# Constant products ahead of TensorE's waits, and the skip path mixed from an image-major load through DRAM, in layer 0 of a two-layer spectral and attention kernel

## Chip, cores and metric

One core of one Trainium2 chip. The metric is the device time of one execution in microseconds (us), as the median over several runs. All arithmetic is in 32-bit floating point.

## What is computed

The input x is [4, 32, 128, 128]: 4 groups b of 32 images t, each 128 rows (w in the kernel) by 128 columns (c). After a group norm over sets of four columns, layer 0 runs on each b: an instance norm, key, query and value made by spectral convolutions with 32 heads, attention over the 32 images of a b, a projection back to one channel with a skip, and two small spectral layers. Layer 1 is a token attention and a mixture of experts; the change does not touch it. The part of the reference that the change touches is the skip inside the attention's values and projection, which for one pixel is a mixing of the 32 images of a b:

```python
def _fno_layer(x, conv_w, skip_w, oh, ow, inner_norm=False, act=False):
    skip = jnp.einsum('bixy,oi->boxy', x, skip_w)
    skip = _fourier_resize(skip, oh, ow)
    xf = _spectral_conv(x, conv_w, oh, ow)
    if inner_norm:
        xf = _inorm(xf)
    y = xf + skip
    ...
v = _fno_layer(xn, Vcw, Vsw, H, W)
...
p_attn = jax.nn.softmax(scores, axis=-1)
av = jnp.einsum('bnts,bnsk->bntk', p_attn, vf)
...
p = _fno_layer(av, Pcw, Psw, H, W)
a = _inorm(p + xa, attn_w, attn_b)
```

## The kernel before

Layer 0 loops over b (line 687). Five engines work on queues of their own, each in its order: TensorE (PE, with its weight loads PEld), VectorE (DVE), ScalarE (ACT), GpSimd (POOL) and SyncE (SP), whose queue issues most of the DMAs. In layer 0 the order of each queue is not the order of the text: the framework's planner takes the text's order as priority, estimates durations, and issues whatever is ready on an engine, so later work can be placed ahead of earlier work that would wait. The order is fixed when the program is built. Layer 1 (line 1020 and after) has its order written out by hand.

Tiles come from pools with tags; tiles of one tag share its buffers. In PSUM the tags are "a", "b" and "wide", two buffers each (a "wide" tile may take two banks). In SBUF the tag "v" has three buffers, "pr" six, and "y", "spec", "rs", "q" one each.

The stages of one b, in the order of the text, with the names that the profile shows:

- Statistics (`image_sums`, line 319). Sums over each image by products with a one-column matrix (`rows8`, line 330), the group norm's mean `gm` and inverse deviation `gr` per column, `gs = gm * gr`, and their copy to every partition, `by_group` (lines 359 to 363): row 0 the scale, row 1 the negative offset, for 32 sets of columns.
- Spectra (`spectra_of_images`, line 418, through `forward`, line 253). Products by line 248 (`pz`) and lines 263 and 264 (`px`), the result to `xx`, and to DRAM as `xd`.
- Scores (`attention_weights`, line 486). For 17 columns yy, two products of elements, `pa` and `pb` (lines 520 to 524, VectorE or GpSimd), and four TensorE products with 32 output rows each into `sp` (line 528). Then a softmax, and the weights to DRAM and back (`prd`, `pr`, lines 572 and 577).
- Product stage (lines 748 to 788). Five blocks x0 of 13 rows of modes (the last 12), and four steps i in each. A step broadcasts a part of `xd` to 128 partitions (`xb`, line 758, four buffers), copies it to PSUM (`xw`, line 767), multiplies it with the weights `gb` four times (`u`, lines 773 on GpSimd and 775 on VectorE) and adds eight products of TensorE into `po` (line 778). Of eight multiplies in two steps, three are GpSimd's. At the end of a block `po` goes to `rs` (line 788).
- Skips (function `skips`, line 719), one piece of 16 columns behind every second step i, eight pieces in the blocks 0 to 3. A piece is 16 transposes on TensorE (`pxt`, line 723), four scalings on ScalarE (`xq`, line 733), four mixing products with the block matrix `bd` (`sk`, line 742), and one copy to `q` (line 745).
- Way back of the attention (`py` line 798, `pv2` line 273, `four` line 278): the result is added to `q` by line 811, eight adds of four images, each with its statistics.
- Two small layers: `spectra(layer, src)` (`pz` line 248, `px` line 871), `weighed` (sums of squares, closed by one product through `sums`, line 314, whose result gives the norm), and `back` (line 288: `y1` line 297, `four` line 308), with an evacuation of `y1` to SBUF between the two. Behind the first layer the exact gelu runs (lines 941 and 944); with it line 848 adds the attention's result. Behind the second, lines 999, 1006 and 1010 finish, and the images go to DRAM (`x1`).

In the text, the statistics of b + 1 stand behind the first small layer of b, its spectra and scores within the second. Before the first b they stand on their own, with the preparation of the weights beside them. `gl`, the gelu's result, and `sqx`, the squares of the first small layer, have the tag "y". The images of b + 1 are loaded at the head of iteration b (`load`, line 120), two transfers on SP's queue and two on ACT's.

## Time and profile before

| | us |
|---|---|
| median of three runs (3177.18 to 3182.71) | 3178.72 |
| profiled execution | 3191.62 |
| its span, first to last instruction | 3189.9 |
| mean granted TensorE clock, share of full | 0.953 |
| TensorE busy | 2928.7 |
| VectorE busy | 2290.9 |
| ScalarE busy | 2311.7 |
| GpSimd busy | 2102.7 |

Layer 0 ends at about 1105 us of the span; its products of line 1010 end there and layer 1's first long run of products starts. The page's second part cuts the span into 40 slices of about 80 us, one digit each: the busy share in tenths, and for PEclk the clock that was granted to TensorE in tenths of full speed. So layer 0 is the first 14 digits. A chain of waits is followed back from the last instruction, at each step to what released it. In a row of groups, "x32" counts instructions; one product of 32-bit operands is two of them in this program (640 products of line 778 are 1280 instructions). "128*32 128x429" is a product with 128 rows of weights, 32 output rows, and 429 columns. A number behind a stage's engine is busy time, and the count of instructions in brackets.

The product stage, from its first `po` product to the last copy `rs`, runs from 113.8 to 181.1 us for b = 0, from 371.5 to 439.8 for b = 1, from 639.0 to 707.5 for b = 2 and from 903.9 to 966.9 for b = 3.

### The profile page before, as it was taken

Reading aid. Unit: us, or ns where it says so; the run is one execution under the profiler, and the core shown is the slowest. Engines: PE = TensorE matmul, PEld = TensorE weight load, DVE = VectorE, ACT = ScalarE, POOL = GpSimd, SP = SyncE. Lnnn points to the kernel's source line nnn. Section 1 sums busy time; section 2 is a strip of 40 time slices with the busy share of each in tenths; the row PEclk is TensorE's granted clock in tenths of the full one; section 3 lists DMA queues with packets and bytes.
Section 4 is the critical chain, followed back from the end, with each engine's and each line's share of the span. In section 5 each row is a group of like instructions: output and inputs, shape, how many; then the busy total and the mean of one; then the engine's idle time right before and its main releaser. Section 6 shows DMA issues by size and latency. Waiting matters only on the chain.

```text
span 3189.9 us, 53099 instructions
## 1 busy us (share of the span) xinstructions
PE 2928.7 (92%) x19634; PEld 1438.2 (45%) x19634; DVE 2290.9 (72%) x5035; ACT 2311.7 (72%) x3138; POOL 2102.7 (66%) x1831
## 2 busy tenths in 40 slices
PE   7888798798888789999999999999999999999997
PEld 5366365345546444444344443444444444444443
DVE  5876666667677566777666868866778777687887
ACT  2344243253343589998999999998999999999992
POOL 1621540460451289878788797889878889888773
PEclk6998998899898799999999999999999999999998
DMA  6301310130140211010111010011010011101000
GB/s 140 111 18 30 95 50 3 49 123 1 30 130 2 57 31 31 8 31 7 31 37 24 14 24 14 8 39 31 23 29 9 14 37 24 37 1 31 14 14 14
DMA packets 152308, 112.77 MB, mean 35 GB/s; under 512 B 36878, under 2 KB 140657, under 8 KB 151441
## 3 DMA queue, kind: packets, MB, share of 16 engines
q1 hardware_dynamic: 136209, 103.61, 12.2%
q10 hardware_dynamic: 15840, 5.77, 0.8%
q8 instruction: 155, 2.54, 0.3%
q14 instruction: 104, 0.85, 0.1%
HBM read 68.37 MB, written 20.00 MB: 28 GB/s over the span
## 4 chain that ended last, share of the span: by engine, by line
PE 61%; POOL 12%; ACT 9%; DVE 9%; issue 7%; DMA 1%; ACTq 0%; POOLq 0%; DVEq 0%; SPq 0%
PE d L1446 19%; PE po L1465 11%; PE px L1352 6%; ACT r L1496 4%; PE po L778 4%; PE n L1446 3%; POOL e L1505 3%; POOL e L1504 3%; PE pz L248 2%; PE four L308 2%; ACT e L1512 2%; PE px L871 1%; PE sk L742 1%; POOL kx L1111 1%; DVE r L1501 1%
## 5 line engine op out<-in xcount | busy, mean ns | idle before, releaser
L1501 DVE TENSOR_TENSOR r<-n,r 128x1024 f32<-128x1024 f32 (+1 forms) x1056 | 961.6, 952 | 479.0 <-PE n L1446 389.4
L1504 POOL TENSOR_TENSOR e<-r 128x512 f32<-128x512 f32 x528 | 673.2, 1275 | 268.1 <-DVE r L1501 267.6
L1496 ACT ACTIVATE r<-d 128x1024 f32<-128x1024 f32 (+1 forms) x1056 | 792.9, 802 | 67.4 <-PE n L1446 56.4
L1508 ACT ACTIVATE r<-r 128x1536 f32<-128x1536 f32 x528 | 783.6, 1484 | 16.8
L1505 POOL TENSOR_TENSOR e<-e,r 128x512 f32<-128x512 f32 x528 | 671.3, 1271 | 41.4
L1446 PE MATMUL d<-qe,ke 32*128 32x512 f32 (+3 forms) x2304 | 605.8, 602 | 39.6 <-ACT r L1496 36.5
L1465 PE MATMUL po<-e,kx 128*128 128x512 f32 (+3 forms) x1152 | 594.5, 605 | 15.6 <-POOL e L1517 15.6
L1446 PE MATMUL n<-qe,ke 32*128 32x512 f32 (+3 forms) x2304 | 606.2, 601 | 0.0
L1446 PE MATMUL n<-qf,kf 32*128 32x512 f32 (+3 forms) x2304 | 552.6, 554 | 0.0
L1446 PE MATMUL d<-qf,kf 32*128 32x512 f32 (+3 forms) x2304 | 550.2, 553 | 0.0
L1356 DVE SCALAR_TENSOR_TENSOR xc<-px,wgt,xc 128x128 f32<-128x128 f32 x1024 | 358.1, 350 | 42.2 <-PE px L1352 9.7
L1512 ACT ACTIVATE e<-e 128x512 f32<-128x512 f32 x528 | 325.8, 617 | 66.2 <-POOL e L1505 65.6
L1465 PEld LDWEIGHTS po<-e,kx 128*128 128x128 f32 x1152 | 175.5, 188 | 392.8 <-issue 306.9
L1446 PEld LDWEIGHTS d<-qe,ke 32*128 32x128 f32 x2304 | 176.5, 183 | 359.3 <-ACT r L1496 339.5
L773 POOL TENSOR_TENSOR u<-xb,gb 128x858 f32<-128x858 f32 (+1 forms) x120 | 233.1, 1968 | 139.5 <-PE po L778 128.0
L1446 PEld LDWEIGHTS d<-qf,kf 32*128 32x128 f32 x2304 | 220.2, 186 | 176.1 <-issue 163.8
L1352 PE MATMUL px<-we,x2t 128*128 128x512 f32 x512 | 264.0, 601 | 6.8 <-DVE xc L1356 6.0
L775 DVE TENSOR_TENSOR u<-xw,gb 128x858 f32<-128x858 f32 (+1 forms) x200 | 206.6, 1082 | 59.2 <-PE po L778 46.6
L885 POOL TENSOR_TENSOR spec<-part,part 128x512 f32<-128x512 f32 x16 | 24.8, 1550 | 333.4 <-ACT z L188 75.2
L1446 PEld LDWEIGHTS n<-qf,kf 32*128 32x128 f32 x2304 | 228.3, 185 | 19.2 <-issue 11.4
L778 PE MATMUL po<-u,pr 128*32 128x429 f32 (+1 forms) x1280 | 191.1, 548 | 26.8 <-DVE u L775 11.7
L524 POOL TENSOR_TENSOR pb<-xm 128x1024 f32<-128x1024 f32 x48 | 90.7, 1913 | 159.1 <-ACT xm L457 152.8
(388 smaller groups left out, 3953.9 us busy)
## 6 DMA issues: line engine op xcount, KB each, us to landing
xb<-xd SPq DMA_DIRECT2D x128, 214.5 KB
xc<-x SPq DMA_DIRECT2D x29, 512.0 KB
x<-x SPq DMA_DIRECT2D x16, 512.0 KB
qf<-qe SPq DMA_DIRECT2D x64, 128.0 KB
out<-xc SPq DMA_DIRECT2D x15, 512.0 KB
xb<-xd SPq DMA_DIRECT2D x32, 198.0 KB
gb<-gd SPq DMA_DIRECT2D x4, 1056.0 KB
x<-in_x SPq DMA_DIRECT2D x8, 512.0 KB
```

The lines of the kernel that those rows point to most:

```text
L773: nc.gpsimd.tensor_tensor(u, xb, gk, ALU.mult)
L778: nc.tensor.matmul(po[32 * j : 32 * j + 32], pr[:, i, k], u[:, r], start=i == 0 and k == 0, stop=i == 3 and k == 1,)
L1352: nc.tensor.matmul(px, x2t[:, k * P : (k + 1) * P], we[:, e0 : e0 + 4], start=True, stop=True)
L1356: nc.vector.scalar_tensor_tensor(xc[:, k], px[:, e], wgt[:, k, e0 + e : e0 + e + 1], xc[:, k], ALU.mult, ALU.add)
L1446: nc.tensor.matmul(o, k, q, start=turn == 0 or g > 0, stop=turn == 1 or g > 0)
L1465: nc.tensor.matmul(sums[c, h][:, q0 : q0 + c1 - c0], kx[:, jb], e[:, c0:c1], start=jb == 0, stop=is_last and q0 > 2 * P, skip_group_check= ...
L1496: nc.scalar.activation(r[:, g], d, AF.Ln, scale=1.0 / DSCALE)
L1501: nc.vector.tensor_tensor(r[:, g], part, r[:, g], ALU.mult)
L1504: nc.gpsimd.tensor_tensor(e, r[:, 1], r[:, 2], ALU.add)
L1505: nc.gpsimd.tensor_tensor(e, e, r[:, 0], ALU.add)
L1508: nc.scalar.activation(r, r, AF.Exp, scale=-1.0)
L1512: nc.scalar.activation(e, e, AF.Exp)
```

## The change

A helper `hold(tile, n)` issues n products of two constant matrices (`rows` and 128 columns of `inv`) into a PSUM tile that nobody reads. They have no input that is computed. The change puts them

- 18 ahead of the product that makes `by_group`, for b = 0;
- 4 ahead of each of the 17 turns of the score loop, into a PSUM tile `beside` of the tag "b";
- 26 and 8 ahead of the two `cm` products, for b = 0, and 14 ahead of the first `po` of every b;
- 24 ahead of the sum that closes `weighed` for `v0`, and for `v1` in the last b;
- 3 in each `back`, ahead of its first `four`.

The skips are made in another way. The group's offset in `by_group` is now the mean alone (`gm`, not `gs`), since the scale is applied afterwards. The images of b are loaded a second time, as `xs`: partition 32 j + t holds rows 32 j to 32 j + 31 of image t, 16 KB of contiguous memory, in four DMAs of 512 KB behind the broadcasts of block 0. A piece is now four rows of each of the four partition groups, all columns: one product of `bd` with 512 columns of `xs`, one of `bd` with the group offsets (read with repetition), and one multiply on VectorE that scales the sum and puts it back in `xs`. The piece goes to DRAM (`qd`, 256 KB), by SP's queue. The eight pieces stand in the blocks 1 to 4. When all are written, `q` is read back in four DMAs of 512 KB; an order without a wait puts them behind the last broadcast of the stage. The load of the images of b + 1 moves from the head of the iteration to behind this read. `xs` has the tag "y".

```diff
--- before.py
+++ after.py
@@ -287,7 +287,6 @@
     def back(spec, a, take):
-
         wide = [ps.tile([P, 2, 512], F32, name="y1", tag="wide") for _ in range(2)]
         for slot in range(4):
             c = slice(slot * P, slot * P + P)
@@ -305,12 +304,22 @@
             v = grp.tile([P, 4, C], F32, name="v1", tag="v", bufs=3)
             evacuate(v.rearrange("p k c -> p (k c)"), wide[g // 2][:, g % 2])
             four = ps.tile([P, 4, C], F32, name="four", tag="b")
+            if g == 0:
+                hold(four[:, 0], 3)
             nc.tensor.matmul(four, inv, v, start=True, stop=True)
             take([image(a, g, k) for k in range(4)], four)
-    def sums(name, matrix, src):
-
-        m = ps.tile(list(src.shape), F32, name=name, tag="wide")
+    def hold(tile, n):
+
+        for _ in range(n):
+            nc.tensor.matmul(tile, rows, inv[:, : tile.shape[-1]], start=True, stop=True)
+
+    def sums(name, matrix, src, idle=0):
+
+        m = ps.tile([P, P] if idle else list(src.shape), F32, name=name, tag="wide")
+        if idle:
+            hold(m, idle)
+            m = m[:, : src.shape[-1]]
         nc.tensor.matmul(m, matrix, src, start=True, stop=True)
         return m
@@ -358,8 +367,10 @@
         both = small.tile([P, 2, 32], F32, name="both", tag="both")
         nc.vector.tensor_scalar(both[:, 0], of_group, gr, None, ALU.mult)
-        nc.vector.tensor_scalar(both[:, 1], of_group, gs, -1.0, ALU.mult, ALU.mult)
+        nc.vector.tensor_scalar(both[:, 1], of_group, gm, -1.0, ALU.mult, ALU.mult)
         by_group = small.tile([P, 2, 32], F32, name="by_group", tag="by_group")
+        if b == 0:
+            hold(ps.tile([P, P], F32, name="early", tag="wide"), 18)
         nc.vector.tensor_copy(by_group, sums("bg", ones, both))
         n = 1 + 2 * KY
         colg = small.tile([P, 2, n], F32, name="colg", tag="colg")
@@ -511,7 +522,9 @@
         )
         sp = ps.tile([P, T, 16], F32, name="sp", tag="b")
+        beside = ps.tile([P, P], F32, name="beside", tag="b")
         for yy in range(KA):
+            hold(beside, 4)
             xs_p = xp[:, yy].unsqueeze(2).to_broadcast(tt)
             xs_s = xm[:, yy].unsqueeze(2).to_broadcast(tt)
             pa = grp.tile(tt, F32, name="pa", tag="pr", bufs=6)
@@ -688,8 +701,6 @@
         xt = loaded
         by_group, _, _, ysc = normed
         xd = front[2]
-        if b + 1 < B:
-            loaded = load(b + 1)
         ph, pr = weights
@@ -700,6 +711,8 @@
         for h in range(2):
             r = slice(32 * h, 32 * h + 32)
             cm = ps.tile([P, T, 16], F32, name="cm", tag="a")
+            if b == 0:
+                hold(cm.rearrange("p s t -> p (s t)")[:, :P], 26 - 18 * h)
             nc.tensor.matmul(cm, pv[r].to_broadcast([NH, P]), ph[r], start=True, stop=True)
             cd = grp.tile([P, T, 16], F32, name="cd", tag="v", bufs=3)
             nc.vector.tensor_tensor(cd, cm, sel.unsqueeze(2).to_broadcast([P, T, 16]), ALU.mult)
@@ -715,47 +728,46 @@
             ALU.mult,
         )
         q = big.tile([P, T, C], F32, name=f"q_{b}", tag="q")
-
-        def skips(c0):
-            px = ps.tile([P, 4, P], F32, name="pxt", tag="a")
-            for k in range(4):
-                for j in range(4):
-                    nc.tensor.matmul(
-                        px[32 * j : 32 * j + 32, k],
-                        xt[:, :, c0 + 4 * k + j],
-                        ident,
-                        start=True,
-                        stop=True,
-                    )
-            xq = grp.tile([P, 4, P], F32, name="xq", tag="v", bufs=3)
-            for k in range(4):
-                g = c0 // 4 + k
-                nc.scalar.activation(
-                    xq[:, k],
-                    px[:, k],
-                    AF.Identity,
-                    bias=by_group[:, 1, g : g + 1],
-                    scale=by_group[:, 0, g : g + 1],
+        rows_of_4 = "t (j w) c -> j t w c"
+        qd = dram.tile([T, H, C], F32, name=f"qd_{b}")
+        xs = big.tile([P, H // 4, C], F32, name=f"xs_{b}", tag="y")
+
+        def load_by_image():
+            for j in range(4):
+                nc.sync.dma_start(
+                    out=xs[32 * j : 32 * j + 32], in_=x[b, :, 32 * j : 32 * j + 32]
                 )
-            sk = ps.tile([P, 16, T], F32, name="sk", tag="b")
-            for k in range(4):
-                nc.tensor.matmul(
-                    sk[:, 4 * k : 4 * k + 4], xq[:, k], bd, start=True, stop=True
-                )
-            nc.scalar.copy(q[:, :, c0 : c0 + 16], sk.rearrange("w c t -> w t c"))
-
-
+
+        def skips(w0):
+
+            r = slice(w0, w0 + 4)
+            sk = ps.tile([P, 4, 32, 4], F32, name="sk", tag="b")
+
+            def over_pixels(t):
+                return t.unsqueeze(1).unsqueeze(3).to_broadcast([P, 4, 32, 4])
+
+            nc.tensor.matmul(sk, bd, xs[:, r], start=True, stop=False)
+            nc.tensor.matmul(sk, bd, over_pixels(by_group[:, 1]), start=False, stop=True)
+            nc.vector.tensor_tensor(
+                xs[:, r].rearrange("p w (g k) -> p w g k", k=4),
+                sk,
+                over_pixels(by_group[:, 0]),
+                ALU.mult,
+            )
+            nc.sync.dma_start(out=qd.rearrange(rows_of_4, j=4)[:, :, r], in_=xs[:, r])
         rs = big.tile([P, KX, KY], F32, name=f"rs_{b}", tag="rs")
-        at_c = 0
+        at_w = 0
         for x0 in range(0, KX, NK):
             nk = min(NK, KX - x0)
             m = nk * KY
             po = ps.tile([P, NK * KY], F32, name="po", tag="a")[:, :m]
+            if x0 == 0:
+                hold(po[:, :P], 14)
             for i in range(4):
                 xb = late.tile([P, 2, NK * KY], F32, name="xb", tag="xb")[:, :, :m]
                 for r in range(2):
-                    nc.sync.dma_start(
+                    last_xb = nc.sync.dma_start(
                         out=xb[:, r],
                         in_=xd[8 * i : 8 * i + 8, r, x0 : x0 + nk]
                         .rearrange("s x y -> s (x y)")
@@ -782,11 +794,25 @@
                                 start=i == 0 and k == 0,
                                 stop=i == 3 and k == 1,
                             )
-                if i % 2 and at_c < C:
-                    skips(at_c)
-                    at_c += 16
+                if x0 and at_w < H // 4:
+                    skips(at_w)
+                    at_w += 4
             nc.scalar.copy(rs[:, x0 : x0 + nk].rearrange("p x y -> p (x y)"), po)
-        if b + 1 == B:
+            if x0 == 0:
+                load_by_image()
+        for g in GROUPS:
+            back_in = nc.sync.dma_start(
+                out=q[:, g : g + GI], in_=qd[g : g + GI].rearrange("t w c -> w t c")
+            )
+            tc.add_manual_dep(
+                back_in.ins,
+                last_xb.ins.name,
+                mybir.DependencyInfo(mybir.DependencyClass.NoSync, mybir.DependencyReason.DATA),
+                reason="order",
+            )
+        if b + 1 < B:
+            loaded = load(b + 1)
+        else:
             for p in reversed(right):
                 p.__exit__(None, None, None)
         yf = big.tile([P, T, 2, KY], F32, name=f"yf_{b}", tag="spec")
@@ -891,7 +917,7 @@
                 nc.scalar.activation(spec[:, s4, :64], spec[:, s4, P:], AF.Copy, scale=-1.0)
             return spec, sq
-        def weighed(name, sq, squares, weights):
+        def weighed(name, sq, squares, weights, idle):
             t = sq[:, 1]
             by_row, by_column = weights
@@ -913,14 +939,14 @@
                 ALU.mult,
             )
             nc.vector.scalar_tensor_tensor(by_t, squares, by_column, by_t, ALU.mult, ALU.add)
-            m = sums("ms", ones, by_t)
+            m = sums("ms", ones, by_t, idle)
             out = per_image(name)
             nc.vector.tensor_copy(out, m)
             return out
         spec, sq = spectra(0, q)
-        v0 = weighed("v0", sq, squares, layers[0][2])
+        v0 = weighed("v0", sq, squares, layers[0][2], 24)
         nc.vector.tensor_mul(v0, v0, r2)
         nc.vector.tensor_mul(v0, v0, r2)
         r0, ve = inv_std("r0", v0)
@@ -967,8 +993,8 @@
         spec, sq = spectra(1, gl)
         if b + 1 < B:
             front = spectra_of_images(b + 1, loaded, normed)
-        v1 = weighed("v1", sq, squares, layers[1][2])
-        vc = weighed("vc", sq, squares, layers[1][3])
+        v1 = weighed("v1", sq, squares, layers[1][2], 24 * (b + 1 == B))
+        vc = weighed("vc", sq, squares, layers[1][3], 0)
         r1, _ = inv_std("r1", v1)
         s1 = par[:, S1 : S1 + 1]
         nc.vector.tensor_mul(vc, vc, r1)
```

## Prediction

> **What bounds the kernel now.** I first read the page's slices, then busy time by stage, then the chain that ended last inside one stage, then the groups of that stage. In the slices the first third of the run (layer 0, to about 1105 us) looks unlike the rest: the granted TensorE clock is often below full.
>
> ```profile
> PE   7888798798888789999999999999999999999997
> DVE  5876666667677566777666868866778777687887
> PEclk6998998899898799999999999999999999999998
> ```
>
> By stage (columns: span, then busy us and count for PE, PEld, DVE, ACT, POOL, then granted clock, DMA share, GB/s):
>
> ```profile
> 32.00:66.00 34.00, 32.41 (x148) 31.64 (x148) 15.72 (x59) 3.43 (x8) 0.00 (x0) 0.50 0.52 114
> 114.00:181.00 67.00, 64.71 (x640) 30.95 (x635) 50.24 (x50) 37.61 (x80) 54.28 (x28) 0.96 0.30 98
> 228.00:238.00 10.00, 9.08 (x73) 5.71 (x76) 8.75 (x41) 3.79 (x7) 0.00 (x0) 0.50 0.00 1
> ```
>
> Here are three kinds of stage. From 32 to 66 us (spectra of the first 32 images, b = 0) TensorE is the bound and runs at half clock, with VectorE idle half the time. From 114 to 181 us (the product stage, lines 748 to 788) it is the bound at full clock. From 228 to 238 us (the way back of the first small layer) TensorE is at half clock but VectorE is nearly full beside it, so a faster TensorE gives only part. The same pair of instructions in the chain, cold and warm, shows what the clock is worth:
>
> ```profile
> 33.25 0.43 PE px L263 x2
> ...
> 282.89 0.22 PE px L263 x2
> ```
>
> One pair of steps i of the product stage, from the chain of b = 1 (start us, us, what):
>
> ```profile
> 397.08 1.69 PE po L778 x17
> 398.77 0.33 PE pxt L723 x3
> 399.10 0.27 PE po L778 x3
> 399.37 0.87 PE pxt L723 x28
> 400.25 0.04 issue
> 400.28 0.91 PE po L778 x2
> 401.19 0.70 PE sk L742 x4
> 401.89 0.85 PE po L778 x6
> 402.74 0.42 PE sk L742 x2
> 403.16 0.84 PE po L778 x2
> 404.00 0.42 PE sk L742 x2
> ```
>
> Nothing but TensorE is on it: 7.34 us, of which po 4.56, the skips' transposes (pxt) 1.20 and their mixing (sk) 1.54. What stands next is read in the groups of 113 to 182 us:
>
> ```profile
> L773 POOL TENSOR_TENSOR u<-xb,gb 128x858 f32<-128x858 f32 (+1 forms) x28 | 54.3, 1970 | 23.6 <-PE po L778 23.1 <-DMA xb<-xd 0.6
> L775 DVE TENSOR_TENSOR u<-xw,gb 128x858 f32<-128x858 f32 (+1 forms) x47 | 49.0, 1090 | 14.4 <-PE po L778 14.3
> ```
>
> A pair has three products on GpSimd (3 x 1.97 = 5.9 us) and five on VectorE (5 x 1.09 = 5.5 us). Both wait for TensorE now, but both are close behind it.
>
> [...] with TensorE idle from 222.3 to 228.6 us the clock falls to 0.50 and stays there to 238, and the pair above takes 0.43 instead of 0.22 us. [...]
>
> **The change, part by part.** The sum is made against the profiled execution (3191.6 us, span 3189.9), which is 0.4% above the median of the runs shown (3178.7); I take the same microseconds off the median.
>
> *Skips, TensorE.* Per piece, 16 transposes and four mixing products go (1.20 + 1.54 = 2.74 us); two products of 512 columns come. The nearest row is the warm four L308: two products in 1.99 us (245.24 us in the chain). So a pair with a piece goes from 7.34 to about 6.6 us. Pieces now lie in blocks 1 to 4 instead of 0 to 3. The last block has none today and takes 10.7 us (170.4 to 181.1), close to its GpSimd products, so block 0 should drop to about 11.5 and the last rise to about 12.5. The stage: 11.5 + 3 x 13.2 + 12.5 = 63.6. A second way: po 10 x 4.56 plus 8 x 1.99 = 61.5 of TensorE alone; VectorE has 50.2 + 8 x 0.68 = 55.7 (a 128x512 add from PSUM, L811, takes 0.68), GpSimd 54.3. I take 62. Now it is 67.3, 68.3, 68.5 and 63.0 us (first po to last rs, b = 0 to 3), so the gain is 5.3 + 6.3 + 6.5 + 1 = **19**. Bounds: 63.6 gives about 13, 58 (GpSimd and VectorE bound) gives 35.
>
> *Skips, ScalarE.* Four xq and one q copy go (4 x 0.46 + 0.59 = 2.4 us a piece). ScalarE is at 37.6 of 67 us: nothing by itself, but TensorE's waits for xq go with it.
>
> *Skips, DMA.* Added per b: 2 MB of xs in, 2 MB of qd out, 2 MB of q in. The stage moves 98 to 136 GB/s now; with 6 MB more in 62 us it is about 200, against 298 to 347 GB/s seen at 4 to 12 us. The xs load is issued behind the first block, but its buffer (tag y) is free long before, so it should lie in front. The q read starts when the last piece is written, about 2.5 us after the stage (the prd write took 2.45). Four reads of 512 KB at about 180 GB/s land 3 us apart: the first at +7, the last at +16 us. The first add into q comes 16 us after the last rs (439.8 to 456.1), hidden by py and pv, and the eight adds take some 12 us more. Cost 0; without that cover about 10 us each. The load of the next images moves from in front of the stage to behind the q read. Today it delays the broadcasts once (9.80 us for one, at 375.9 us, little of it in block 0's 13.9 us); it is wanted only 70 us later. I count nothing.
>
> *New waits on SP's queue.* Each qd write waits for its multiply, and the broadcasts queued behind it wait too, on them the copies, the products and po. Four broadcast buffers, about 13 us ahead, cover it if the planner keeps later broadcasts in front of the write. I count 0; not below, since a wait adds nothing.
>
> *Group bias.* both[:,1] needs gm instead of gs: it executed at 30.36 us though gr came at 25.2, so TensorE's by_group product (30.64) can start earlier: **-1.5**.
>
> *Constant products, b = 0.* One constant product is a 128-column pair: 0.22 us warm (as px), 0.43 cold. Eighteen fill 4 us between 23 and 30.6 us, where the clock fell. Then 32.4 us of cold work becomes 16.2, with VectorE's 15.7 partly behind it; b = 1 needs about 22 us for this, part of it cold. 34 to 21: **-13** (-6 if VectorE's order binds, -16 at best). The 26, 8 and 14 products around cm and po fill 101 to 113 us, where TensorE is idle anyway: **-1.5** from a cold first pair.
>
> *Constant products before v0.* Twenty-four (5.3 us) fit the 6.3 us of waiting. Cold work behind it: b = 1 has 20.6 us of it from 493.0 to 513.7, half of which is 10; beside VectorE I take 7. b = 0: 9.6 us cold, but VectorE 8.75 of 10 busy: 2.5. b = 2: only 771 to 777 us: 2. b = 3: 3.5. **-15** (0 to -24). Those ahead of v1 in the last b come before a 13 us wait of TensorE: 0. The three per way back fit in the 0.6 us evacuation: 0.
>
> *Constant products in the score loop (line 528).* 17 x 4 x 0.22 = 15 us of TensorE. For b = 0 the loop is VectorE's (27 us, 1.4 a turn), and 0.9 + 1.1 us a turn is more: **+5**. For b = 1 to 3 GpSimd sets it (34 us, four 2.37 us additions in it): +1 each. **+8** (0 to +25).
>
> Sum: -19 - 1.5 - 13 - 1.5 - 15 + 8 = **-42**: 3149.6 for the profiled execution, **3137** for the median.
>
> **Rivals.**
> *No gain in the product stage.* With GpSimd at 5.9 and VectorE at 5.5 + 0.7 a pair, the in-order queues may lock at 7 us. Then -42 + 19 = -23: 3156. For it: both are within 1.5 us of TensorE; against it: both wait on po, 23.1 and 14.3 us.
> *Constant products spent early.* They have no inputs, and the planner moves ready work forward (sc of line 540 runs at 70.35 us, ahead of line 528's products at 72.2). If they are spent in small gaps, the long waits stay cold: -42 + 13 + 1.5 + 15 = -12: 3166. Against it for b = 0: TensorE has little else between 23 and 30 us.
> *More clock than counted.* All cold bounds and GpSimd-bound product stages: -35 - 19 - 24 = -78: 3101.
> *Slower: SP's queue.* If the qd writes stand in front of the next broadcasts, each of 32 pieces exposes part of a broadcast's landing. Its bounds are 2.0 us (the pr read) and 9.8 us (broadcast under load). At 3 us, +96 - 42 = +54: 3233. It decides from 42/32 = 1.3 us a piece. Against it: broadcasts are issued four buffers ahead now, and ready work goes first.
>
> **How the numbers follow.** Forecast 0.58; no stage gain 0.15; spent early 0.07; more clock 0.09; slower 0.08; balanced to nothing 0.03. About 0.2% (6 us) is what a measurement tells from no change. Range 3098 to 3175: it takes in all but the slower case and the nought. Faster 0.89, same 0.03, slower 0.08.
>
> **What would show it.** Right: clock 1.0 between 32 and 60 us with px pairs at 0.22; product stages of 60 to 64 us with pairs near 6.5; no wait of the q additions on a DMA; a score loop of b = 0 near 32 us. Wrong: broadcasts that land after their copies are due and SP waiting for the multiply (slower rival); pairs still above 7 us with GpSimd on the chain; clock 0.50 still at 228 or 485 us.

## The result, and the profile after

The changed kernel is **slower**, by 1.2%: 3214.44 us (median of four runs, 3213.43 to 3230.11) against 3179.22 us (median of four, 3177.18 to 3182.71); ratio 1.0121 [1.0089, 1.0153]. Here and below a ratio is to the kernel before, run beside the other, and the brackets hold its 95% interval. The profiled execution took 3230.11 us (span 3228.3), 15.7 above its median; that of the kernel before lies 12.4 above its own. So stages of the two traces may be set side by side, but a difference of some 10 us in one place needs a second trace. The mean granted TensorE clock of the profiled execution rose from 0.953 to 0.971, and the time rose too.

The slices of after. The first third has more clock than before, and TensorE is busier in it:

```profile
PE   7989989988998889999998999999999999999997
PEclk8999999999999899999999999999999999999998
```

The same three kinds of stage after the change (span, then busy us and count for PE, PEld, DVE, ACT, POOL, then clock, DMA share, GB/s):

```profile
37.00:64.00 27.00, 26.05 (x174) 25.75 (x174) 15.46 (x56) 5.67 (x10) 0.00 (x0) 0.75 0.55 118
131.00:199.00 68.00, 57.22 (x350) 14.34 (x344) 50.16 (x54) 21.25 (x41) 51.36 (x28) 0.92 0.52 166
246.00:256.00 10.00, 7.27 (x80) 4.58 (x80) 9.70 (x45) 5.99 (x13) 0.00 (x0) 0.93 0.00 0
```

In the product stage TensorE's work did fall, from 64.71 to 57.22 us, and ScalarE's from 37.61 to 21.25. But the stage took 68 us as before: TensorE now idles in it, and its clock falls to 0.92. The way back (third line) has its clock, and VectorE is full, 9.70 of 10 us.

The chain through the product stage of b = 1, where the piece shown before was TensorE alone, now has three broadcasts in it:

```profile
397.56 10.84 DMA xb<-xd
...
410.75 1.88 POOL u L785
412.62 0.04 issue
412.67 0.91 PE po L790 x4
...
427.49 1.48 DMA qd<-xs
...
430.98 11.02 DMA xb<-xd
...
448.11 10.03 DMA xb<-xd
```

The first of the three was issued ahead of every write of qd of this b (the first is at 412.11 us), behind the writes of the finished images of b = 0 (x<-x) and two loads of the next images. The planner still put these loads in front of most broadcasts (at 396.44 us), though in the text they now stand behind the read of q. The kernel before had such a broadcast too (9.80 us at 375.9 us). The other two stand among the writes of qd, and are new.

The groups of 130 to 200 us, the stage of b = 0 (busy us, mean ns of one, then idle us and what ended it), say who waits: ScalarE's copies xw, for broadcasts, 28.4 us in this one stage.

```profile
L785 POOL TENSOR_TENSOR u<-xb,gb 128x858 f32<-128x858 f32 (+1 forms) x28 | 51.4, 1857 | 33.2 <-PE po L790 29.4 <-DMA xb<-xd 2.7 <-DVE u L787 0.9
L787 DVE TENSOR_TENSOR u<-xw,gb 128x858 f32<-128x858 f32 (+1 forms) x46 | 45.5, 1031 | 14.8 <-ACT xw L779 8.6 <-PE po L790 6.0
L779 ACT COPY xw<-xb 128x429 f32<-128x429 f32 (+1 forms) x34 | 17.4, 515 | 48.9 <-DMA xb<-xd 28.4 <-DVE u L787 20.2
```

The second loss is in the score loop. The chain of b = 1 from the end of the spectra; "beside" is the tile of the constant products:

```profile
322.83 3.81 PE beside L315 x18
326.64 2.06 PE so L514 x30
...
328.76 2.88 PE beside L315 x24
331.64 1.00 PE sp L541 x8
332.63 0.42 PE beside L315 x2
333.05 0.99 PE sp L541 x8
...
337.07 1.31 PE beside L315 x10
```

TensorE is the whole chain up to the last sp product, which ends at 366.8 us. From the first sp product (331.64 us) its pieces add up to 20.8 us of sp and 14.0 us of constant products; the loop had taken 31.7 us.

By stages, summed over the four b, the two traces differ as in the first two rows below; the other rows are the experiments of the next section. "Time" is the median in us, the rest is read from the one trace of each kernel. "Score" is from the last px product of the spectra to the last sp product; "to po" from there to the first po product (b = 0 alone); "stage" from the first po to the last rs; "back" from there to the last px of the next b (of b = 3 to the end of layer 0).

| kernel | time | score | to po, b = 0 | stage | back |
|---|---|---|---|---|---|
| before | 3179 | 145.4 | 16.4 | 272.3 | 522.5 |
| after | 3214.4 | 179.7 | 23.0 | 284.5 | 508.4 |
| e1 no constants in the loop | 3195.6 | 149.0 | 20.1 | 284.5 | 504.7 |
| e2 no constants | 3199.4 | 146.3 | 22.1 | 289.6 | 506.4 |
| e3 constants only | 3202.7 | 177.3 | 22.1 | 268.3 | 499.3 |
| e4 qd by partition | 3207.9 | 177.9 | 22.9 | 253.5 | 522.9 |
| e5 qd on ScalarE's queue | 3224.3 | 177.8 | 23.0 | 284.4 | 501.1 |
| e6 broadcast on 16 | 3195.6 | 177.3 | 23.0 | 254.2 | 501.6 |
| e7 fast qd, fewer constants | 3164.8 | 142.7 | 27.2 | 256.7 | 502.1 |
| e8 constants but in the loop | 3176.2 | 147.2 | 19.2 | 263.7 | 502.4 |
| e9 half the loop's constants | 3198.7 | 157.9 | 18.5 | 288.2 | 498.1 |
| e10 skips alone, fast qd | 3165.6 | 144.2 | 20.8 | 255.7 | 506.0 |
| e11 e7, xs behind pr | 3159.9 | 144.3 | 16.4 | 261.5 | 508.6 |
| e12 e11, broadcast on 16 | 3166.7 | 144.3 | 16.3 | 259.0 | 504.3 |
| e13 first constants alone | 3180.6 | 143.8 | 20.3 | 271.6 | 503.5 |
| e14 e13 and ahead of my | 3182.5 | 142.4 | 26.6 | 269.9 | 508.7 |
| e15 e11 without constants | 3171.4 | 145.3 | 22.9 | 266.7 | 506.0 |

The kernel before, run beside each set, had medians of 3179.9 (e1 to e4), 3176.5 (e5 to e8), 3178.5 (e9 to e12) and 3183.9 us (e13 to e15); so kernels of different sets are compared by their ratios. Layer 1 takes 2084 to 2089 us in every trace. Of the 37.9 us that layer 0 ends later after the change, 34.3 are the score loops, 12.2 the stages, 6.6 the way to po of b = 0, 0.7 the same of the other b; -1.8 the first spectra, -14.1 the ways back.

### The profile page after: what moved, and what is told of

Its sections match the earlier page's. It is cut to its first block, busy times and chain, and to the rows that moved or that the text cites. A ratio compares the mean times of both kernels' runs of the same rounds, so it can differ in the third digit from the quotient of the medians.

```text
span 3228.3 us, 52967 instructions
## 1 busy us (share of the span) xinstructions
PE 3017.4 (93%) x19578; PEld 1484.6 (46%) x19578; DVE 2303.7 (71%) x5067; ACT 2249.0 (70%) x2978; POOL 2092.1 (65%) x1831
## 4 chain that ended last, share of the span: by engine, by line
PE 63%; POOL 11%; DVE 9%; ACT 8%; issue 5%; DMA 4%; SPq 0%; ACTq 0%; POOLq 0%; DVEq 0%
PE d L1472 18%; PE po L1491 11%; PE px L1378 6%; ACT r L1522 4%; PE n L1472 3%; DMA xb<-xd 3%; PE pz L248 3%; POOL e L1531 3%; PE sp L541 3%; POOL e L1530 3%; PE beside L315 2%; PE four L309 2%; PE po L790 2%; POOL u L785 2%; PE px L897 2%
## 5 line engine op out<-in xcount | busy, mean ns | idle before, releaser
L1522 ACT ACTIVATE r<-d 128x1024 f32<-128x1024 f32 (+1 forms) x1056 | 792.8, 802 | 68.4 <-PE n L1472 56.4
L1538 ACT ACTIVATE e<-e 128x512 f32<-128x512 f32 x528 | 325.8, 617 | 66.1 <-POOL e L1531 65.4
L785 POOL TENSOR_TENSOR u<-xb,gb 128x858 f32<-128x858 f32 (+1 forms) x120 | 221.6, 1866 | 174.4 <-PE po L790 109.3
L779 ACT COPY xw<-xb 128x429 f32<-128x429 f32 (+1 forms) x160 | 82.3, 515 | 240.5 <-DMA xb<-xd 122.7
L787 DVE TENSOR_TENSOR u<-xw,gb 128x858 f32<-128x858 f32 (+1 forms) x200 | 197.4, 1031 | 56.1 <-ACT xw L779 38.8
L1472 PEld LDWEIGHTS n<-qf,kf 32*128 32x128 f32 x2304 | 228.2, 185 | 19.1 <-issue 11.4
L790 PE MATMUL po<-u,pr 128*32 128x429 f32 (+1 forms) x1280 | 176.4, 579 | 48.1 <-POOL u L785 33.0
```

The lines of the kernel that those rows point to most:

```text
L785: nc.gpsimd.tensor_tensor(u, xb, gk, ALU.mult)
L790: nc.tensor.matmul(po[32 * j : 32 * j + 32], pr[:, i, k], u[:, r], start=i == 0 and k == 0, stop=i == 3 and k == 1,)
L1472: nc.tensor.matmul(o, k, q, start=turn == 0 or g > 0, stop=turn == 1 or g > 0)
L1522: nc.scalar.activation(r[:, g], d, AF.Ln, scale=1.0 / DSCALE)
L1538: nc.scalar.activation(e, e, AF.Exp)
```

## Experiments

The theory ahead of the runs: the score loop became TensorE's through the constant products, and the product stage waits for broadcasts because the writes of qd and the broadcasts share few DMA engines. Its rivals: the constant products cost little and disturb in another place; SP's queue in order holds the broadcasts back; the bytes are too many.

**e1: the loop's constant products taken out.**

```diff
-        beside = ps.tile([P, P], F32, name="beside", tag="b")
         for yy in range(KA):
-            hold(beside, 4)
```

> The changed kernel without the four constant products a turn in the score loop (line 528). Theory (they stand on the chain of a loop that TensorE now sets; the four loops took +12.3, +6.5, +8.1 and +7.4 us): about 34 us come back, 3180, level with the kernel before; the loop of b = 0 ends about 28 us after its first products, as before. Rival (the loops are longer for another cause, the later start of the work ahead or VectorE's order, and the products only fill gaps): under 8 us, 3207 to 3215.

Measured: 3195.58 us, 1.0047 [1.0031, 1.0062]. The theory holds for the loops: they are back at 149.0 us, 30.7 less in the traces. In time it does not hold in full: 18.9 us come back in the medians, of some 34 expected. So the loop is a large loss, but with it gone 15.7 us remain: there is a second one.

**e2: the new skips without any constant product; e3: the constant products on the kernel before.**

```diff
-            hold(beside, 4)
...
-            hold(ps.tile([P, P], F32, name="early", tag="wide"), 18)
...
-                hold(cm.rearrange("p s t -> p (s t)")[:, :P], 26 - 18 * h)
...
-                hold(po[:, :P], 14)
...
-                hold(four[:, 0], 3)
...
-        v0 = weighed("v0", sq, squares, layers[0][2], 24)
+        v0 = weighed("v0", sq, squares, layers[0][2], 0)
```

(e3 has the opposite lines, put into the kernel before.)

> The changed kernel with all constant products taken out, in every place; the new skips stay. What the new skips are worth alone against the kernel before. Theory (the writes of qd and the broadcasts share few DMA engines, the stages give +0.7, +6.2, +2.8, +3 us): slower than before by 8 to 16 us, 3187 to 3195. Rival (it is the constant products that moved the stages into a worse order, and the skips gain the 19 us of the forecast): 3160.

> The kernel before with all constant products put in, its own skips kept. Theory (score loops +34, cm and po of b = 0 about +5, against some -2 for the first spectra and -6 for the way back of layer 0): about +25 to +31 us, 3204 to 3210. Rival (the constant products pay for themselves as in the forecast, -13 -1.5 -15 + 8 = -21): 3158.

Measured: e2 3199.39 us, 1.0057 [1.0037, 1.0078], its stages 289.6 us; e3 3202.68 us, 1.007 [1.005, 1.009], its loops 177.3 us. Each half of the change loses by itself, some 20 us each. The mechanisms of the theory are seen in both; in time e2 lost more than the range said (19.5 us) and e3 a little less (22.8 us).

**e4: qd laid out as the partitions of xs.**

```diff
-        qd = dram.tile([T, H, C], F32, name=f"qd_{b}")
+        qd = dram.tile([P, H // 4, C], F32, name=f"qd_{b}")
...
-            nc.sync.dma_start(out=qd.rearrange(rows_of_4, j=4)[:, :, r], in_=xs[:, r])
+            nc.sync.dma_start(out=qd[:, r], in_=xs[:, r])
...
-        for g in GROUPS:
-            back_in = nc.sync.dma_start(
-                out=q[:, g : g + GI], in_=qd[g : g + GI].rearrange("t w c -> w t c")
-            )
+        for j in range(4):
+            js = slice(32 * j, 32 * j + 32)
+            back_in = nc.sync.dma_start(out=q[js], in_=qd[js].rearrange("t w c -> w t c"))
```

> The changed kernel with qd laid out as the partitions of xs have it (128 rows of 16 KB), so that a write's outer dimension is 128 and not 4; q is read back in four reads by band of rows, not by images. The bytes, the instructions that multiply and the waits of SP's queue are the same. Theory (a write whose outer dimension is 4 runs on 4 DMA engines, and the broadcasts beside it on 8, the same ones among them, so that these few are full while the mean share is 0.43): the product stages fall by 2 to 6 us each, 8 to 20 in all, 3195 to 3206, and the mean DMA share of the stage falls less than the broadcasts' landing does. Rival (SP's queue in order: the broadcasts behind a write wait for its multiply): no change within 4 us, perhaps +3 to +8 because the first addition into q now waits for all four reads.

**e5: the write of qd from ScalarE's queue.**

```diff
-            nc.sync.dma_start(out=qd.rearrange(rows_of_4, j=4)[:, :, r], in_=xs[:, r])
+            nc.scalar.dma_start(out=qd.rearrange(rows_of_4, j=4)[:, :, r], in_=xs[:, r])
```

> The changed kernel with the 32 writes of qd issued from ScalarE's queue instead of SP's; their layout stays (outer dimension 4). No broadcast stands behind a write's wait any more, but the bytes and the DMA engines that they need are the same. Theory (few DMA engines): the product stages stay long, within 3 us each of the changed kernel's 68.0, 74.5, 71.3 and 70.7 us, and the copies wait for broadcasts as much as before; 3208 to 3220. Rival (SP's queue in order holds the broadcasts back): the stages fall to 61 to 66 us, as they did with the other layout, 3185 to 3190.

**e6: broadcasts with an outer dimension of 16.**

```diff
-                        .unsqueeze(1)
-                        .to_broadcast([8, 16, m]),
+                        .unsqueeze(0)
+                        .to_broadcast([16, 8, m]),
```

(with gb and pr in the same order of partitions)

> The changed kernel with the order of the partitions of xb, gb and pr turned (head outside, image inside), so that a broadcast's source has an outer dimension of 16 with step 0 and not of 8; pr is read in 8 pieces instead of 2. qd's layout stays. Theory (few DMA engines): if the stepless outer dimension of 16 spreads a broadcast over 16 engines, the broadcasts' part on the four engines of the qd writes halves, the stages fall by 4 to 8 us each, 3190 to 3200; if the spread goes by something else, nothing. Rival (the bytes themselves, 150 to 180 GB/s, are what the stage can get): no change within 5 us.

Measured: e4 3207.9 us, 1.0082 [1.0057, 1.0106]; e5 3224.28, 1.0164 [1.0144, 1.0184]; e6 3195.55, 1.0061 [1.004, 1.0082]. In time e4 and e5 lie somewhat above their ranges, e6 within. The stages in sum: 253.5, 284.4 and 254.2 us against 284.5. What the copies xw waited for between 100 and 1015 us (count, then busy and mean ns, then idle and what ended it), one fence each for after, e4, e5 and e6:

```profile
L779 ACT COPY xw<-xb 128x429 f32<-128x429 f32 (+1 forms) x160 | 82.3, 515 | 240.5 <-DMA xb<-xd 122.7 <-DVE u L787 73.7 <-DVE pa L535 36.1
```

```profile
L778 ACT COPY xw<-xb 128x429 f32<-128x429 f32 (+1 forms) x159 | 81.5, 516 | 152.3 <-DVE u L786 127.1 <-DMA xb<-xd 16.6 <-issue 3.8
```

```profile
L779 ACT COPY xw<-xb 128x429 f32<-128x429 f32 (+1 forms) x159 | 81.6, 516 | 203.9 <-DMA xb<-xd 122.0 <-DVE u L787 78.5 <-DVE v L190 2.1
```

```profile
L780 ACT COPY xw<-xb 128x429 f32<-128x429 f32 (+1 forms) x159 | 81.5, 516 | 151.6 <-DVE u L788 113.9 <-DMA xb<-xd 29.6 <-issue 3.8
```

The wait for broadcasts (DMA xb<-xd) is 122.7 us, and stays 122.0 when the writes leave SP's queue, but falls to 16.6 or 29.6 when the shape of either transfer changes with its bytes unchanged. This clears SP's queue (e5) and the bytes (e4, e6). What is left is how a transfer is spread over the DMA engines.

The trace has no column by engine, but it has the start and the duration of every DMA packet, so the packets in flight can be counted, here every 0.02 us and where none but those of qd writes and broadcasts are in flight. From 143 to 199 us of after, with packets of a qd write (outer dimension 4) alone in flight, there are 4 of them in 236 of 254 samples. Of the broadcasts (outer dimension 8) alone, in the product stage of b = 0 of the kernel before, 8 is the most frequent count. With both in flight in after it is 8 again, in 514 of 1028 samples, and hardly ever more than 10; on engines of their own they would often be 12 (4 and 8, an estimate from these counts). So by the counts they share, as e4's expectation had it. In e4 a write (outer dimension 128) has up to 15 packets in flight, and in e6 broadcasts alone (16) have most often 16. In the views this is the DMA share, the last number but one: 0.28 with a write alone and 0.52 with both (after), 0.48 with a broadcast alone (before). Of the 16 engines that the share is a mean of, these are 4.5, 8.3 and 7.7. The traces go no further: what sets the number of engines of a transfer, and which ones it gets, was not shown.

```profile
157.80:159.00 1.20, 1.20 (x12) 0.23 (x4) 1.01 (x2) 0.30 (x1) 0.49 (x1) 1.00 0.28 104
173.30:174.80 1.50, 0.93 (x8) 0.16 (x8) 1.15 (x2) 0.00 (x0) 1.50 (x2) 1.00 0.52 163
166.08:166.94 0.86, 0.86 (x4) 0.23 (x2) 0.65 (x1) 0.00 (x0) 0.86 (x1) 1.00 0.48 179
```

Widening either transfer is enough: each gave 30 us in the stages, more than was expected of e4 and within what was expected of e6. The mean share over a longer stretch hides all this: in after the stretch 143 to 188 us, full of waits for DMA, shows a share of only 0.44 at 155 GB/s; in e4, 136 to 180 us, it is 0.58 at 182 GB/s with few of them.

e4's time fell by 6.5 us only, since "back" rose to 522.9 us. In e4 all four reads of q are due before the first addition. No addition waits for a DMA in its trace, but their order is another: for b = 0 the first comes 14.9 us behind the last rs, 12.5 in after. With the reads in 16 pieces (e7) "back" is 502.1 us; that the reads set the order is likely, and not shown by itself.

**e7: the fast qd (the layout of e4), read back by band and images in 16 pieces, no constants in the loop nor around cm and po.**

```diff
-        for g in GROUPS:
+        for g, j in ((g, j) for g in GROUPS for j in range(4)):
+            js = slice(32 * j, 32 * j + 32)
+            ts = slice(32 * j + g, 32 * j + g + GI)
             back_in = nc.sync.dma_start(
-                out=q[:, g : g + GI], in_=qd[g : g + GI].rearrange("t w c -> w t c")
+                out=q[js, g : g + GI], in_=qd[ts].rearrange("t w c -> w t c")
             )
...
-            hold(beside, 4)
...
-                hold(cm.rearrange("p s t -> p (s t)")[:, :P], 26 - 18 * h)
...
-                hold(po[:, :P], 14)
```

> The changed kernel with qd by partition (as in the run before), read back in 16 pieces by band and images so that the first addition waits for four of them, and without the constant products in the score loop and around cm and po; those of the first spectra and of the way back stay. Theory: from 3208 (qd by partition, read by band) the loops give back about 31, the products around cm and po of b = 0 about 2, the read by images about 10 of the 17 us that the ways back of layer 0 had lost: 3160 to 3172, faster than the kernel before by 0.3 to 0.6%. Rival (the gains overlap: GpSimd and VectorE set the score loop and the stage, and only part comes back): 3175 to 3190, no gain over the kernel before.

Measured: 3164.77 us, 0.9959 [0.9948, 0.997], as the theory said: 0.4% faster than the kernel before, "back" at 502.1 us. Yet b = 0 took 27.2 us to its first po. The chain there:

```profile
105.42 9.32 DMA prd<-ph
...
114.83 2.58 DMA pr<-prd
117.42 0.00 issue
117.42 2.05 PE sk L744 x2
119.47 3.00 PE po L783 x13
```

The write of prd took 2.45 us in the kernel before. Three of the four loads of xs stand on SP's queue ahead of it, and a skip's product stands ahead of the first po.

**e10: the new skips alone, with the fast qd.** The edit is e7's, with all constant products out.

> The new skips without any constant product, with qd by partition, read back in 16 pieces. It tests the forecast's -19 for the product stage with the few DMA engines out of the way. Theory: the stages are those of the forecast, 61 to 66 us, 10 to 20 us in sum below the kernel before, of which b = 0 gives 5 back ahead of its first po (the load of xs stands in front of ph's round trip): 3163 to 3172. Rival (the constant products, not the layout, made the short stages of the last runs): 3180 or more.

Measured: 3165.61 us, 0.996 [0.9951, 0.997]; stages 62.0, 63.5, 64.1 and 66.1 us. This comes close to the forecast's product stage (62), without a single constant product. It also prices the products that e7 still has, at the first spectra and in the ways back: the mean clock is 0.968 in the median of e7 and 0.958 in that of e10, and the ratios are the same.

**e11: xs and the next images behind; e12: with the broadcasts on 16.**

```diff
+                tc.add_manual_dep(
+                    by_band.ins,
+                    last_pr.ins.name,
...
+            tc.add_manual_dep(
+                first.ins,
+                last_po.ins.name,
...
-            loaded = load(b + 1)
+            loaded = load(b + 1, last_xb)
```

(order on the queues only, no waits; by_band is the load of xs, first a skip's first product; the two reads of pr also change queues, so that the last one is on SP's)

> The kernel with qd by partition and no constant products in the loop nor around cm and po, and in addition the loads of xs put behind the read of pr, the load of the next images behind the last broadcast, and the first product of a skip behind the last po product ahead of it in the program. Theory (in b = 0 the write of prd took 9.32 us beside the loads of xs, 2.45 in the kernel before, and a skip's product of 2.05 us stood ahead of the first po): b = 0 gives 7 to 9 us, the rest nothing: 3154 to 3160. Rival (the stages get longer because the skips start later and the DMA has more to do within them): 3160 to 3170.

> The run before it on this list, with the broadcasts on an outer dimension of 16 as well. Theory (with qd off the few engines nothing waits for a broadcast any more; the stages are GpSimd's, VectorE's and TensorE's): within 4 us of it. Rival (broadcasts on 8 engines still bound the stage): 4 to 12 us faster.

Measured: e11 3159.86 us, 0.9948 [0.9931, 0.9964], the lowest ratio of all, though its interval overlaps those of e7 and e10; e12 3166.73, 0.9966 [0.9955, 0.9978]. In e11 b = 0 needs 16.4 us to po, as in the kernel before, but the stages grow by 4.8 us against e7: a broadcast behind the loads takes 9.43 us. Theory and rival both hold in part. e12's median is 6.9 us above e11's, not within 4, but the intervals overlap; the broadcasts on 16 add nothing that can be told once qd is spread.

**e9: half the loop's constant products.**

```diff
-            hold(beside, 4)
+            hold(beside, 2)
```

> The changed kernel with two constant products a turn in the score loop instead of four. From the last px product to the last sp product the four batches took 145.4 us in sum in the kernel before and 179.7 after. Theory (in the loop of b = 1 TensorE has 20.3 us of sp products and 14.9 us of constant ones, 35.2, against 31.7 us that GpSimd needs; half the constant ones give 27.8, so GpSimd sets b = 1 to 3 again, and only the products ahead of the loop and b = 0, where VectorE needs 25, still cost): 150 to 156 us in sum. Rival (each constant product costs the same wherever it stands): 162 us in sum. In time: 3192 to 3200 against 3199 to 3206.

Measured: 3198.73 us, 1.0066 [1.0043, 1.009]; score 43.5, 37.8, 38.5 and 38.1 us, 157.9 in sum, above the theory's 150 to 156, through b = 0. For b = 1 to 3 this is the kernel before (37.9, 38.1, 37.8): GpSimd, busy all through these loops (28.2 of 28.2 us), sets their end again, and the half that is left is free. The tile `beside` is still there, so it was not the buffer that it takes. For these loops the cost has a threshold and is not a price a piece. b = 0 did not follow, and TensorE's order in e9 says why:

```profile
80.60 0.49 PE L315 MATMUL cm<-cst 128*128 128x128 f32 x2
81.02 0.62 PE L541 MATMUL sp<-pa,w_re 128*32 128x512 f32 x2
...
92.97 1.60 PE L315 MATMUL cm<-cst 128*128 128x128 f32 x12
```

The products meant for cm have no computed inputs, and the planner put 29 of the 34 into this loop. In e1 and e8, without any product meant for the loop, all but two moved likewise, in front of the loop of b = 0 or into it, and its score is 5.4 and 4.2 us above the kernel before; in after none did.

**e8: the constant products, but for the loop's, on the kernel before** (e3 with the line of e1 taken out).

> The kernel before with its own skips and all constant products but those in the score loop. It tests the forecast's -13 (first spectra) and -15 (way back) without the loop's cost. Theory (the way back gains about 14 us, as the stages of the run with all constant products show, 296 against 311 us in sum; the first spectra end 6 us earlier but VectorE, busy 25.5 of 26 us in the loop behind them, takes most of it back; cm and po of b = 0 cost about 6): -8 to -14, 3166 to 3172. Rival (the forecast: -13 -1.5 -15 = -29): 3150. Rival (the constants give nothing beyond what they cost): 3178 to 3182.

Measured: 3176.24 us (20 runs), 0.9988 [0.9975, 1.0001]: at most a quarter of a percent gained, perhaps nothing. Theory and forecast both fail; the rival that the constants give nothing beyond what they cost comes nearest. Layer 0 in before and in e8 (the clock is the third number from the end):

```profile
0.00:1105.60 1105.60, 934.24 (x7868) 563.73 (x7868) 764.94 (x1928) 433.14 (x915) 395.65 (x216) 0.87 0.21 59
```

```profile
0.00:1092.50 1092.50, 965.45 (x8420) 598.52 (x8420) 767.10 (x1928) 434.11 (x915) 395.90 (x216) 0.93 0.22 59
```

The clock rises from 0.87 to 0.93, and the median time hardly follows. In the trace the ways back are 20.1 us shorter and the stages 8.6, but from the last sp to the first po it takes 18.0 us more over the four b. Which of this is the products' doing isn't shown.

**e13: the first 18 products alone; e14: with 36 more ahead of my.** In the changed kernel TensorE's order in b = 0 was

```profile
22.70 4.26 PE L315 MATMUL early<-cst 128*128 128x128 f32 x36
26.80 0.33 PE L323 MATMUL bg<-both,ones 128*128 128x64 f32 x2
26.97 1.33 PE L248 MATMUL pz<-cst,x 128*128 128x128 f32 x10
35.91 0.66 PE L323 MATMUL my<-y,ones 128*128 128x64 f32 x2 [7.60 <-DVE y L396]
```

The long wait, 7.60 us, comes behind the products. In the kernel before TensorE had waited 4.47 us right ahead of bg, where they now stand.

```diff
+        if b == 0:
+            hold(ps.tile([P, P], F32, name="early2", tag="wide"), 36)
         my = sums("my", ones, y12)
```

> The kernel before with only the 18 constant products ahead of the group norm's second product (bg), b = 0. Theory (the long wait is the one for my, which comes behind them): the px products are still at 0.43 us a pair for their first third, the spectra end 4 to 6 us earlier than before (65.8), the score loop of b = 0 ends 3 to 5 us earlier; in time -5 to 0. Forecast: spectra end 13 us earlier.

> The run before it on this list with 36 further constant products ahead of my, where TensorE waited 7.60 us in the changed kernel: at 0.22 us each they fill 8 us. Theory (that wait is what lets the clock fall): px pairs at 0.22 us from the start, the spectra end at 53 to 56 us, 10 to 13 us earlier than before; but the score loop behind, where VectorE is busy 25 of 26 us, ends at 90 to 93 us, at most 7 us earlier: in time -7 to -2. Rival (the clock falls for another reason than that wait): px pairs at 0.43 us in the first third as in the run before it, and the same end.

Measured: e13 3180.62 us, 0.999 [0.9978, 1.0003], spectra to 60.4 us; e14 3182.45 us, 0.9995 [0.9985, 1.0005], spectra to 56.4. In e14 the clock is 1.00 from 32 to 56 us and the spectra take 21 us, which is the forecast's own figure; so that wait is what let the clock fall. The times show no change that can be told, against 2 to 7 us expected of e14. Its score loop ends at 87.6 us, 9.8 earlier than before, and the first po comes at 114.2 (before: 113.8). The chain of e14:

```profile
71.97 11.01 DMA xd<-xx
...
90.68 6.37 DMA xb<-xd
97.08 0.04 issue
97.12 0.52 ACT xw L779
97.64 0.52 ACT spt L548
98.16 0.04 issue
98.21 1.91 PE sc L559 x2
```

The copy of the scores (spt) stands behind two copies xw on ScalarE's queue; these wait for the first broadcasts, and they stand on SP's queue behind the last writes of xd, seventeen small loads and two of the next images. That DMA chain sets the pace of b = 0, not the spectra.

**e15: e11 without constants.**

> The fastest kernel so far (qd by partition, xs behind the read of pr, 3160 us) without any constant product. Theory (the constant products that are left raise the clock but not the pace, which VectorE and GpSimd set): within 5 us of it, 3155 to 3165. Rival (they are worth the forecast's 13 and 15 us where nothing else is in the way): 3180 or more.

Measured: 3171.41 us, 0.996 [0.9944, 0.9975]; e11 had 0.9948 [0.9931, 0.9964]. The median lies between the ranges of theory and rival, and the intervals overlap: no worth of the constant products can be told. The first po of b = 0 comes at 110.1 us in both traces.

One thing in this trace qualifies e13 and e14. Without any constant product, it has its first spectra at full clock from 45 us and ends them at 55.8, earlier than e13. e2, also without any, has TensorE's work in the same order and with the same waits up to there (4.66 us ahead of the first px in both), and stays at half clock beyond 66 us. The stretch 48 to 56 us in e15 and in e2:

```profile
48.00:56.00 8.00, 8.00 (x73) 7.89 (x72) 4.48 (x15) 1.26 (x3) 0.00 (x0) 1.00 0.50 101
48.00:56.00 8.00, 8.00 (x39) 8.00 (x39) 2.49 (x7) 1.26 (x3) 0.00 (x0) 0.50 0.48 101
```

So part of what one trace shows of the spectra is chance. Only e14 never loses the clock there; with the first 18 products it is back at 44 to 47 us in every trace, without them at 45 in one and at 75 to 79 us in three.

## Why the prediction was wrong

Forecast -42, measured +35. In the traces layer 0 ends 37.9 us later, so the forecast missed by 80 us: 31 in the product stage, 26 in the score loop, 11 in the first spectra, 9 around cm and po, and little elsewhere. Two steps failed above all: "Skips, DMA ... Cost 0", and the size of the score loop.

- **Product stage, -19.** The step that failed is "Skips, DMA ... Cost 0". It compared the bytes of the stage with the most that had been seen (200 against 298 to 347 GB/s). A rate summed over 16 engines can't show that a few of them are wanted twice: a qd write alone had 4 packets in flight, a broadcast alone 8, and both together 8. In its place: +12.2 us in the traces, and 31 us back by a change of layout (e4). Other parts of that step were right: no addition into q waits for a DMA in after. TensorE's term was right in kind: where nothing else is in the way the stages take 62.0 to 66.1 us (e10), 16.6 us less in sum. The start of the stage of b = 3 had been misread: the first po product is at 898.73 us, not 903.9, so the stage was 68.2 us and not 63.0, and 62 us a stage would have been -24.

```profile
898.73 0.93 PE L778 MATMUL po<-u,pr 128*32 128x429 f32 x8 [1.81 <-DVE cd L705]
```

- **SP's queue, 0.** Right: with the writes on another queue the broadcasts are as late as before (e5). So the slower rival falls, though it came nearest in size (3233) and its sign, late broadcasts, did appear.
- **Score loop, +8.** The mechanism was named and its size missed: +34.3. A turn of TensorE was nearly right (0.9 + 1.1 = 2.0 us against 35.2 / 17 = 2.07). Three other terms failed. The cover for b = 1 to 3 was put at 34 us of GpSimd; the loop had taken 31.7, and the three loops grow by 3.6, 5.1 and 4.2 us to 35.2 to 36.8. For b = 0 the step had 2.0 us a turn against VectorE's 1.4 and still wrote +5; the loop grew from 25.2 to 35.2, +10. And 21 of the 68 products stand ahead of the loop, which was counted at nothing: 11.4 us over the four b. These cost only because the loop behind them is TensorE's own: in e9 the same 21 stand there, the loops of b = 1 to 3 start some 3 us later than in the kernel before, and they end as early. Half as many products would have been free in b = 1 to 3 (e9). In the medians the loop's products cost 19 us (e1 against after), by the ratios of e3 and e8 26.
- **First spectra, -13.** In the traces -1.8. Two steps failed. The 18 products fill the wait ahead of bg (4.47 us before), but a wait of 7.60 us then stands behind them and the clock falls there. And only VectorE was asked for as what may bind next ("-6 if VectorE's order binds"); with the spectra at full clock (e14) the first broadcasts are late next, and no gain can be told.
- **Around cm and po, -1.5.** +6.6 in its place. Not foreseen: beside the moved load of xs the round trip of ph is longer (5.66 + 3.02 us in e2, 2.45 + 2.03 before), and a skip's product of 2 us stands ahead of the first po. The constant products alone delay it as much (e3): the 14 ahead of po take 5.76 us and end at 124.4, while the read of pr was issued at 117.8 us and takes some 2.
- **Before v0, -15.** The ways back are 14.1 us shorter, but 16.5 shorter without any constant product (e10). So the near hit is luck: the gain is not theirs, and the trace of before, which lies 12.4 us above its median, had an unusually long one (b = 1). The clock does rise there as forecast (0.93 for 0.50), but beside a VectorE that is busy 9.70 of 10 us.
- **both from gm, -1.5.** Not measured by itself. In e2 bg does come earlier (27.90 us, 30.64 before), but the first px comes at 33.00 (before: 32.13), so nothing is gained in that trace.
- **The clock's return.** That the clock falls in a wait is in the traces (in the kernel before it is 0.50 from 226 to 238 us, in a wait of 6.34 us that ends at 228.57 and behind it). What brings it back was not shown: from 48 to 66 us of that kernel TensorE is busy 18.00 of 18 us, and the clock stays at 0.50.
- **The other rivals.** "No gain in the product stage" (GpSimd and VectorE lock at 7 us a pair) is refuted by e10. "Constant products spent early" was no cause in the changed kernel, but e9 shows that the planner does it where it finds room.

What stays open: why 31 us in the loops become 19 in the medians (e1). The mean clock fits: it is 0.967 in the median of e1's runs and 0.978 in that of after, and among executions of the kernel before 0.01 of mean clock goes with 13 to 19 us. That the loop's products keep the stages behind them at a higher clock would explain it; this was not shown.

## What to carry to other kernels

Before a DMA is called free, look at the outermost dimension of its side in DRAM (4 or 128 in e4, 8 or 16 in e6) and at what else runs in the same stretch: a mean share of 0.44 went with writes of 4 packets in flight and broadcasts of 8 that had 8 together. A constant product is free only while its engine has slack against the next limit of that very loop (two a turn were free in b = 1 to 3 in e9, four were not); count the engine's whole work there, from the chain, and expect a planner to move an instruction without inputs. When a stall is removed, follow the chain to what comes last next before a gain is booked. A clock that constant products raise is not a gain by itself (e7 against e10).

## What the runs showed of the hardware that was not expected

- The order of two dimensions in a broadcast (8 outside or 16 outside, same bytes) moved the waits for it from 122.7 to 29.6 us. A write with an outer dimension of 4 had 4 packets in flight in 236 of 254 samples, a broadcast with 8 had 8 most often, and both together 8 in half of the samples.
- One wait of 7.6 us put TensorE at half clock although it had been busy just before: px pairs at 0.43 us until 44 us and 0.22 from 48.4, some 10 us of work later. Filling that one wait kept the clock at 1.00 (e14).
- How long the clock stays at half is not set by TensorE's work alone: with the same order of work and the same waits, it was back at 45 us in e15 and not by 66 us in e2.
- Constant products between real ones cost 0.30 us each (14.0 us for 47 on the chain of b = 1) and not the 0.23 that they take in a row (18 from 22.70 to 26.80 us).
- Executions of the kernel before spread from 3169 to 3202 us over the sets, the faster ones with the higher mean clock (0.950 to 0.963), so one trace can't settle 10 us.
